# Node-number products for two tiles at once, fewer semaphore waits on VectorE, and shorter ties between gathers and VectorE in a two-layer graph network on one core

## The chip, the cores and the metric

The kernel runs on one core of a Trainium2 chip. The metric is the time of the whole program on the device in microseconds. The core's engines are TensorE (PE in the profile; PEld is its weight loading), VectorE (DVE), ScalarE (ACT), GpSimd (POOL) and SyncE (SP). Each has its own queue of instructions and works through it in order; they wait for each other through semaphores. GpSimd issues the indirect DMAs (gathers), SP most other DMAs.

## The reference

6250 nodes of 256 features, 106250 edges sorted by their target node (100000 random ones and a loop for each node). Layer one is a relational message layer, layer two a graph attention layer of four heads; each is added to its input and normalised.

```python
# layer one
S = feat[src]
msgs = edge_nn(S, W_rel[rel], b_rel[rel])        # relu(relu(S W^T + b) W^T + b), two relations
agg = segment_sum(msgs, dst)
gates = agg @ W_ih.T + b_ih + b_hh               # i, f, g, o
hn = sigmoid(o) * tanh(sigmoid(i) * tanh(g))
x1 = layernorm(x + mlp(hn))                      # W1, W2, W3
# layer two (edges of x1, and a second loop for each node)
h = (x1 @ W).reshape(n, 4, 64)
e = leaky_relu(a_src[src] + a_dst[dst], 0.2)
ex = exp(e - segment_max(e, dst)[dst])
alpha = ex / (segment_sum(ex, dst)[dst] + 1e-16)
out = segment_sum(h[src] * alpha, dst)
y = relu(layernorm(out + bias + x1) * ln_gamma + ln_beta)
return layernorm(x1 + y)
```

## The kernel before

**Tiles, windows, groups, pairs.** The 100000 edges other than the loops are cut into 782 tiles (`TC`) of 128 edges, one edge a partition. Seven tiles (`WT`) make a window, two windows a group (`NG` groups, 56). A group's edges end in at most 128 consecutive nodes. The first window's seven tiles fall into the lower 64 of them (`low_s`), the last four into the upper 64 (`high_s`), and the three between (`MID`, tiles 7 to 9) into any. A group also looks at the first tile of the next one, so it has `GS` = 15 tiles. Groups go in pairs through layer two's weights; the last four go alone.

**Layer one** (in `fast`, from line 1847). For each tile GpSimd gathers 128 rows of 256 numbers from a table of finished messages into a buffer `G`, and TensorE sums them to their target nodes as a product with a one-hot matrix (`sum0`, L2175, accumulated in `fps`). When a group is summed, `turn` (VectorE L1924, L1928; TensorE's transposes L1939; VectorE's copy L1942 to `faT`) hands it to `update`, which runs the gates and the dense layers for up to four groups, and stores the rows of layer two. For the first six groups, ten of the fourteen tiles have been gathered before the loop begins (60 gathers, L1605); only four tiles a group come late.

**Layer two** (from line 2256). GpSimd gathers a row of 260 numbers for each tile (features and the four logits of the source node) into `G[w]`. ScalarE copies the logits out (L2626, L2618). `ahead` makes each edge's node numbers: SP loads the pair's target slots, repeated on every partition (`dB`), VectorE compares them with the partition's number (`ohT`, L2338, 128 x 1920 in bf16), TensorE multiplies each of the 15 tiles' 128 x 128 of `ohT` with the group's `node3` (three bf16 parts of eight numbers a node, 24 columns; L2345), and VectorE adds the three parts (L2355). `weights` turns logits into attention weights through running maxima (L2385 to L2409). `weighted` (L2424, L2429, L2430) multiplies the gathered rows by the weights into `gw`, TensorE sums `gw` by node (L2546), and `finish` normalises and stores a group (L2444 to L2495).

**The order.** Each layer is one loop over steps; a step issues one gather, then the summing of the tile four steps back (`LAG`), then `run.step()`, in which chains of work (`turn`, `update`, `ahead`, `weights`, `finish`) go on by one piece each; a `yield n` in a chain means "n steps later". What is written first stands first in an engine's queue. A step in layer one has the number n of its gather in the loop, which starts at n = 60; in layer two it has the tile's number t, and gathers begin at t = 21.

**The ties.** GpSimd's gathers would run ahead as far as the buffers let them. `Pace` ties them: after each step it notes the last VectorE instruction written so far (`passes`), and `hold(move, n, ahead)` makes gather n wait for the instruction noted `ahead` steps earlier. In layer one `ahead` is `AHEAD0`; in layer two it is `AHEAD1` plus the larger of 0, 42 - (t - 21) // 6 and 21 - (782 - t) // 2 (L2602), so that the tie starts 42 steps looser and tightens until t = 273, and loosens again over the last 42 tiles.

**VectorE's waits for gathers.** `gw` (L2430) reads a window's seven gathered tiles. Each of those gathers signals one of eight semaphores, and L2430 waits for them. The logits of these same rows have gone through ScalarE (L2626) and the whole chain of `weights` before.

Of the kernel before, what the change touches and what calls it, by code (L numbers as in the profile page):

```python
# [42 lines left out]
P = 128  # L43
# [3 lines left out]
H = 4  # L47
# [17 lines left out]
BF16 = mybir.dt.bfloat16  # L65
WT = 7
# [3 lines left out]
GS = 2 * WT + 1  # L70
# [14 lines left out]
AHEAD_G = range(AHEAD_W // 2)  # L85
LATE = 3
CR = 16 * WT
AHEAD0 = 2 * WT
AHEAD1 = WT + 1
NOROW = NP + P // 2 - 1  # L90
SORTED = "the fast path runs only where the chip has found the edges sorted"

# [1547 lines left out]
def fast(  # L1640
# [46 lines left out]
    def at(ap, offset, dims):  # L1687
        return bass.AP(tensor=ap.tensor, offset=ap.offset + offset, ap=dims)
# [35 lines left out]
    class Steps:  # L1724
# [18 lines left out]
        def finish(self):  # L1743
            while self.chains:
                self.step()
# [510 lines left out]
    with (  # L2256
# [45 lines left out]
        def ahead(pair, box):  # L2302

            cut = ring(ep, [P, P + 1], F32, "cut", 3)
            of = ring(ep, [P, 2 * GS, 2 * H], F32, "of", 3)
            box.update(cut=cut, of=of)
            i0, n = pair[0] % 2, len(pair)
            if i0 == 0:
                box["dB"] = ring(ep, [P, 2, GS * P], BF16, "dB", 1)
            else:  # L2310
                box["dB"] = boxes[pair[0] - 1]["dB"]
            dB = box["dB"][:, i0 : i0 + n, :]
            nc.sync.dma_start(
                dB.rearrange("p i e -> p (i e)"),
                at(slots, pair[0] * GS * P, [[0, P], [1, n * GS * P]]),
            )
            if pair in pairs[:2]:
                for i, g in enumerate(pair):
                    nc.sync.dma_start(
                        cut[i * GS * H : (i + 1) * GS * H, :],  # L2320
                        at(cuts, tiles_in(g)[0][0] * P, [[P, GS], [0, H], [1, P + 1]]),
                    )
            else:
                o = pair[0] % 2 * GS * H
                n = ((len(pair) - 1) * GS + len(tiles_in(pair[-1])[1])) * H
                pc = ring(tps, [P, P + 1], F32, "turn", 2)
                nc.tensor.matmul(
                    pc[:n, :],
                    pick[:, pair[0] % 8 // 2, o : o + n],
                    cut_all[:, pair[0] // 8, :],  # L2330
                    start=True,
                    stop=True,
                )
                nc.scalar.copy(cut[:n, :], pc[:n, :])
            yield 12 if len(pair) > 1 else 8
            for i, g in enumerate(pair):
                ohT = ring(ep, [P, GS, P], BF16, "ohT", 2)
                nc.vector.tensor_scalar(  # L2338
                    ohT.rearrange("p j e -> p (j e)"), dB[:, i, :], iota_p, None, op0=OP.is_equal
                )  # L2340
                yield 2
                n = len(tiles_in(g)[1])
                pn = ring(ops, [P, GS, 3, 2 * H], F32, "pn", 2)
                for j in range(n):
                    nc.tensor.matmul(  # L2345
                        pn[:, j, :, :].rearrange("p c a -> p (c a)"),
                        ohT[:, j, :],
                        node3[:, g, :, :].rearrange("p c a -> p (c a)"),
                        start=True,
                        stop=True,  # L2350
                    )
                    if j == WT:
                        yield 1
                yield 1
                nc.vector.tensor_reduce(  # L2355
                    of[:, i * GS : i * GS + n, :],
                    pn[:, :n, :, :].rearrange("p j c a -> p j a c"),
                    axis=AX.X,
                    op=OP.add,
                )  # L2360
                yield 1
# [56 lines left out]
        def weighted(g, w, o, n, of, ex, top):  # L2418

            if g not in ohs:  # L2420
                ohs[g] = ring(ep, [P, (2 * WT - 2) * LOW + 3 * P], F32, "oh1", 2)
                one_hot(ohs[g], g, slot, MID[1])
            gw = ring(ep, [P, WT if n > 1 else 1, D + 2 * H], F32, f"gw{min(n, 2)}", 4)[:, :n, :]
            nc.vector.tensor_mul(  # L2424
                gw[:, :, HA:],
                top[:, o : o + n, :],
                first[:, WT * w : WT * w + n, None].to_broadcast([P, n, H]),
            )
            nc.scalar.copy(gw[:, :, D:HA], ex[:, o : o + n, :])  # L2429
            nc.vector.tensor_mul(  # L2430
                gw[:, :, :D].rearrange("p j (h f) -> p j h f", h=H),
                of[:, :n, :D].rearrange("p j (h f) -> p j h f", h=H),
                ex[:, o : o + n, :, None].to_broadcast([P, n, H, F]),
            )
            return gw

        def finish(g, ps):
# [73 lines left out]
        pair_of = {g: p for p in pairs for g in p}  # L2511
        boxes = {p[0]: {} for p in pairs}
        sums, queue, read, ohs, k3s, left, written = {}, [], set(), {}, {}, {}, []
        results = {}

        def sum1():

            while late and len(queue) < 8:
                piece = late.pop(0)
                g, w, o, n = piece[:4]  # L2520
                gw = weighted(*piece)
                queue.extend((g, WT * w + j, gw[:, j, :]) for j in range(n))
            if not queue:
                return
            g, t, gw = queue[0]
            if g not in sums and g >= 2 and g - 2 not in read:
                return
            queue.pop(0)
            if g not in sums:
                sums[g] = ring(eps, [P, D + 2 * H], F32, "fps1", 2)  # L2530
                left[g] = len(tiles_in(g)[1])
                u = everyone
                if g % 2 == 0:
                    k3s[g // 2] = ring(fp, [P, 2, 3, D], F32, "k3", 2)
                of = k3s[g // 2].rearrange("p i c f -> p i (c f)")
                if len(pair_of[g]) == 1:
                    nc.sync.dma_start(of[:, g % 2, :], kept[g // 2, :, g % 2, :])
                elif g % 2 == 0:
                    nc.sync.dma_start(of, kept[g // 2])
            begins = left[g] == len(tiles_in(g)[1])  # L2540
            left[g] -= 1
            j = t - 2 * WT * g
            to, cols = place(j, MID[1])
            ohj = ohs[g][:, cols]
            ends = left[g] == 0 or j in (WT - 1, TC - 1 - 2 * WT * g)
            nc.tensor.matmul(sums[g][to, :], ohj, gw, start=begins, stop=ends)  # L2546
            if left[g] == 0:
                run.start(finish(g, sums[g]), 1)

        def aheads():  # L2550
            for pair in pairs:
# [42 lines left out]
        while t < TC + LAG or late or queue or run.chains:  # L2594
            if EARLY <= t < TC:
                w = t // WT
                if t % WT == 0:
                    G[w] = ring(rowsp, [P, WT * HA], F32, "G", 10).rearrange(
                        "p (j f) -> p j f", f=HA
                    )  # L2600
                move = gather(G[w][:, t - WT * w, :], rows1, idx1[:, t : t + 1])
                pace.hold(move, t, AHEAD1 + max(0, 6 * WT - (t - EARLY) // 6, 3 * WT - (TC - t) // 2))  # L2602
            k = t - LAG
            if 0 <= k < TC:
                if k < EARLY:
                    complete(k)
                w = k // WT
                g = w // 2
                pair = pair_of[g]
                box = boxes[pair[0]]  # L2610
                if k % (2 * WT) == 0:
                    if g == pair[0]:
                        box["e"] = ring(ep, [P, 2 * GS, H], F32, "e", 3)
                    if g:

                        old = pair_of[g - 1]
                        ob = boxes[old[0]]
                        nc.scalar.copy(  # L2618
                            ob["e"][:, old.index(g - 1) * GS + 2 * WT, :], G[w][:, 0, D:HA]
                        )  # L2620
                        if old is not pair:
                            run.start(weights(old, ob))
                if k == tiles_of(w)[0][-1]:
                    o = pair.index(g) * GS + WT * (w % 2)
                    own = len(tiles_of(w)[0])
                    nc.scalar.copy(box["e"][:, o : o + own, :], G[w][:, :own, D:HA])  # L2626
                    if w == NW - 1:
                        run.start(weights(pair, box))
            sum1()
            if len(queue) + W8 * len(late) > 3 * W8 or t % 7 == 0 or t >= TC - 4 * WT:  # L2630
                sum1()
            run.step()
            pace.passes()
            t += 1
# [62 lines left out]
```

## Time and profile before

| | |
|---|---|
| median of 9 runs | 2182.18 us (2180.41 to 2187.76) |
| the profiled execution | 2182.2 us, its span 2180.4 us |
| granted TensorE clock, mean | 0.843 (0.96 from 237 to 1131 us, 0.71 to 0.74 after 1159 us) |

Busy microseconds of each engine in four stretches (layer one's gathers; layer two until 1500 us; the rest of its gathers; the tail):

| stretch, us | PE | DVE | ACT | POOL |
|---|---|---|---|---|
| 237 to 1131 | 775.1 | 364.6 | 216.5 | 678.3 |
| 1159 to 1500 | 207.2 | 260.8 | 61.2 | 256.0 |
| 1500 to 2131 | 361.0 | 499.6 | 125.5 | 478.4 |
| 2131 to 2181 | 18.6 | 33.5 | 10.4 | 0.0 |

A profile row for a group of instructions gives its line, its engine, its operation, what it writes and reads, and a count; then busy us, mean ns of one, and the idle time of the engine just before these instructions with what ended it. A row of the timeline gives start and duration in us, and in square brackets the idle time before it and what ended it; "issue" is time in which the engine waited for nothing that the profile shows. A row of the chain gives start, duration and the work that the end was waiting for.

### The profile page before, as it was taken

To read this page: it belongs to the slowest core of one execution; us is meant where nothing else is said; L and a number is where in the kernel's file an instruction comes from. 1 tells how busy PE (TensorE), PEld (TensorE's weight loads), DVE (VectorE), ACT (ScalarE), POOL (GpSimd) and SP (SyncE) were. 2 spreads that over 40 slices of the span, in tenths; PEclk is the share of its full clock that TensorE was granted. 3 is DMA by queue.
4 is the path that set the end of the run, shared out by engine and by line. 5 is a ranking of instruction groups with operands and counts; after the bars stand their busy time and mean duration, and the time that the engine had idled before them with its cause. 6 is when DMAs were issued, how large, how long until landed. Compare 5 with 4: busy or idle time off the path is not lost.

```text
span 2180.4 us, 23269 instructions
## 1 busy us (share of the span) xinstructions
PE 1587.1 (73%) x6390; PEld 849.6 (39%) x6390; DVE 1319.2 (61%) x3622; ACT 499.4 (23%) x1538; POOL 1543.8 (71%) x1610
## 2 busy tenths in 40 slices
PE   8988998788888888788886665565564656555554
PEld 5656543333333333333454333233332333333332
DVE  8854354434343433434443788888887777778786
ACT  3333132122221222122351121221211112121212
POOL 2465677777777777777777777777777777777770
PEclk9999999999999999999996776777776767676777
DMA  5356645455554555445555555655555555555551
GB/s 158 118 170 174 188 145 184 140 145 172 169 166 122 165 167 167 137 148 173 185 156 175 164 166 161 178 161 158 181 162 160 164 160 164 160 170 153 164 160 38
DMA packets 146105, 346.12 MB, mean 159 GB/s; under 512 B 36154, under 2 KB 66720, under 8 KB 145965
## 3 DMA queue, kind: packets, MB, share of 16 engines
q0 software_dynamic: 76048, 207.99, 34.7%
q1 hardware_dynamic: 67741, 133.51, 17.7%
q10 hardware_dynamic: 2176, 3.05, 0.4%
q8 instruction: 52, 0.85, 0.2%
q14 instruction: 88, 0.72, 0.1%
HBM read 291.90 MB, written 52.52 MB: 158 GB/s over the span
## 4 chain that ended last, share of the span: by engine, by line
PE 27%; DVE 22%; DMA 18%; issue 11%; POOL 9%; ACT 5%; DVEq 0%; POOLq 0%; ACTq 0%
DMA G<-parts,fidx 10%; PE fps L2175 9%; POOL G L1717 9%; DMA G<-rows,fidx 8%; DVE gw L2430 5%; PE fpg L2006 5%; PE fps L2546 4%; DVE oh L1832 4%; PE fpg L2092 2%; PE fps L2288 1%; PE fpm L1571 1%; DVE fst L2476 1%; PE fpg L2054 1%; ACT fy L2484 1%; DVE ohT L2338 1%
## 5 line engine op out<-in xcount | busy, mean ns | idle before, releaser
L1717 POOL DMA_INDIRECT G<-rows,fidx x761 | 730.5, 960 | 235.2 <-issue 130.9
L1717 POOL DMA_INDIRECT G<-parts,fidx x722 | 693.4, 960 | 230.5 <-issue 156.0
L2546 PE MATMUL fps<-gw,oh 128*64 128x264 f32 (+1 forms) x1674 | 472.0, 472 | 187.9 <-DVE gw L2430 187.9
L2175 PE MATMUL fps<-G,oh 128*64 128x257 f32 (+1 forms) x1674 | 495.3, 413 | 123.3 <-DMA G<-parts,fidx 108.7
L2546 PEld LDWEIGHTS fps<-gw,oh 128*64 128x64 f32 (+1 forms) x1674 | 243.4, 178 | 335.9 <-DVE gw L2430 202.5
L2175 PEld LDWEIGHTS fps<-G,oh 128*64 128x64 f32 (+1 forms) x1674 | 207.9, 154 | 388.7 <-DMA G<-parts,fidx 187.6
L2430 DVE TENSOR_TENSOR gw<-G,bank 128x1792 f32<-128x1792 f32 (+1 forms) x167 | 248.9, 1490 | 57.6 <-ACT gw L2429 52.9
L2006 PE MATMUL fpg<-faT,fWihT 128*128 128x512 f32 (+2 forms) x432 | 171.1, 520 | 0.2 <-DVE faT L1942 0.2
L1832 DVE TENSOR_TENSOR oh<-bank,fslot 128x448 f32<-128x448 f32 (+2 forms) x318 | 156.5, 547 | 8.9 <-ACT bank L2409 5.8
L1924 DVE TENSOR_SCALAR kind<-fps 128x1 f32<-128x1 f32 x112 | 12.4, 152 | 214.2 <-PE fps L2175 214.2
L1571 PE MATMUL fpm<-fWrT,fhT 128*128 128x256 f32 x392 | 94.6, 393 | 13.1 <-DVE fms L1579 13.1
L2126 DVE COPY nd<-hr 128x4 f32<-128x4 f32 x53 | 9.7, 184 | 152.6 <-ACT hr L2098 152.6
L2006 PEld LDWEIGHTS fpg<-faT,fWihT 128*128 128x128 f32 x432 | 71.3, 191 | 67.2 <-issue 56.4
L1557 PE MATMUL fph<-fxc,fWrT 128*128 128x512 f32 (+1 forms) x208 | 89.9, 582 | 5.4 <-DMA fWrT<-in_WrT_dram 4.6
L1605 POOL DMA_INDIRECT G<-parts,fidx x60 | 61.2, 1019 | 43.2 <-DVE fms L1579 18.9
L2345 PE MATMUL pn<-node,ohT 128*128 128x24 bf16 x837 | 41.0, 180 | 67.6 <-DVE ohT L2338 67.6
L1571 PEld LDWEIGHTS fpm<-fWrT,fhT 128*128 128x128 f32 x392 | 75.3, 196 | 32.0 <-DVE fms L1579 11.8
L2478 ACT ACTIVATE frs<-fmv,eps_c 128x1 f32<-128x1 f32 x112 | 32.9, 294 | 238.5 <-DVE gw L2424 153.2
L2484 ACT ACTIVATE fy<-fy,frs 128x256 f32<-128x256 f32 x112 | 66.9, 597 | 87.1 <-DVE frs L2481 86.9
L2345 PEld LDWEIGHTS <-ohT 128*128 128x128 bf16 x837 | 34.1, 103 | 109.0 <-DVE ohT L2338 75.4
L2378 PE MATMUL turn<-fident,e 128*120 128x128 f32 (+2 forms) x30 | 11.6, 388 | 88.2 <-ACT e L2618 88.2
L2092 PE MATMUL fpg<-Wx,fyT 128*128 128x264 f32 x224 | 71.2, 445 | 3.0 <-ACT fyT L2083 3.0
(348 smaller groups left out, 1969.9 us busy)
## 6 DMA issues: line engine op xcount, KB each, us to landing
dB<-slots SPq DMA_DIRECT2D x26, 960.0 KB, 6.1
kept<-keep SPq DMA_DIRECT2D x26, 768.0 KB, 5.2
k<-kept SPq DMA_DIRECT2D x26, 768.0 KB
loop<-parts SPq DMA_DIRECT2D x55, 256.0 KB, 2.9
parts<-fms SPq DMA_DIRECT2D x49, 256.0 KB, 2.4
G<-parts,fidx POOLq DMA_INDIRECT x782
G<-rows,fidx POOLq DMA_INDIRECT x761
out_dram<-fy SPq DMA_DIRECT2D x56, 128.0 KB, 2.9
```

What stands on the lines that cost most here:

```text
L1557: nc.tensor.matmul(ph[:, :cols], WrT_s[:, r, k, m * P : (m + 1) * P], xc[:, k, :cols], start=(k == 0), stop=(k == 1),)
L1571: made = nc.tensor.matmul(pm[:, r, :], hT[:, r, k, j * P : (j + 1) * P], WrT_s[:, r, k, :], start=(k == 0), stop=(k == 1),)
L1605: nc.gpsimd.indirect_dma_start(out=of[:, n % WT, :D], out_offset=None, in_=parts0[: 2 * P * block, :], in_offset=bass.IndirectOffsetOnAxis ...
L1717: return nc.gpsimd.indirect_dma_start(out=to_tile, out_offset=None, in_=table, in_offset=bass.IndirectOffsetOnAxis(ap=idx, axis=0),)
L1832: nc.vector.tensor_tensor(to[:, o : o + len(js) * n].rearrange("p (j s) -> p j s", s=n), iota_s[:, None, cols].to_broadcast([P, len(js), n ...
L2006: nc.tensor.matmul(pg[:, :cols], WihT_s[:, k, c * P : (c + 1) * P], aT[:, k, :cols], start=(k == 0), stop=(k == 1),)
L2092: nc.tensor.matmul(ph[u, :], hs[i][:, k, u], Wx[:, k, :], start=(k == 0), stop=(k == 1))
L2175: nc.tensor.matmul(sums[g][to, :], ohj, got[t], start=begins, stop=ends)
L2345: nc.tensor.matmul(pn[:, j, :, :].rearrange("p c a -> p (c a)"), ohT[:, j, :], node3[:, g, :, :].rearrange("p c a -> p (c a)"), start=True ...
L2430: nc.vector.tensor_mul(gw[:, :, :D].rearrange("p j (h f) -> p j h f", h=H), of[:, :n, :D].rearrange("p j (h f) -> p j h f", h=H), ex[:, o ...
L2484: nc.scalar.activation(y, y, AF.Identity, bias=m, scale=r)
L2546: nc.tensor.matmul(sums[g][to, :], ohj, gw, start=begins, stop=ends)
```

## The change

Three edits.

1. **Products for two tiles.** `dB` and `ohT` hold 10 tiles' columns instead of 15. Columns 0 to 4 hold, in the lower 64 partitions, tiles 0 to 4 and, in the upper 64, tiles 10 to 14; columns 5 and 6 hold tiles 5 and 6 below and -1 above; columns 7 to 9 hold tiles 7 to 9 in all partitions. The load of `dB` becomes three, each to 64 partitions. For each group ScalarE copies `node3` into `node2[g % 4]`, a matrix of 48 columns whose first 24 are zero above and whose last 24 are zero below. One product of a column of `ohT` with it writes the results of tiles j and j + 10. A group has 10 products instead of 15 (five of 48 columns, five of 24), split 6 and 4 by the `yield`. Four `node2` buffers are zeroed and `dB` is filled with -1 once, at the start of layer two.
2. **VectorE's waits.** L2430's dependence on the gathers of its window is declared absent.
3. **Ties.** `AHEAD0` from 14 to 7, `AHEAD1` from 8 to 5.

```diff
-AHEAD0 = 2 * WT
-AHEAD1 = WT + 1
+AHEAD0 = WT
+AHEAD1 = WT - 2
...
-                box["dB"] = ring(ep, [P, 2, GS * P], BF16, "dB", 1)
+                box["dB"] = ring(ep, [P, 2, MID[1] * P], BF16, "dB", 1)
...
-            nc.sync.dma_start(
-                dB.rearrange("p i e -> p (i e)"),
-                at(slots, pair[0] * GS * P, [[0, P], [1, n * GS * P]]),
-            )
+            for ps, c0, j0, jn in (
+                (low_s, 0, 0, MID[1]),
+                (high_s, 0, MID[1], GS - MID[1]),
+                (high_s, MID[0], MID[0], MID[1] - MID[0]),
+            ):
+                nc.sync.dma_start(
+                    dB[ps, :, c0 * P : (c0 + jn) * P],
+                    at(slots, (pair[0] * GS + j0) * P, [[0, LOW], [GS * P, n], [1, jn * P]]),
+                )
...
-                ohT = ring(ep, [P, GS, P], BF16, "ohT", 2)
+                halves = node2[g % 4]
+                for h, ps in enumerate((low_s, high_s)):
+                    nc.scalar.copy(
+                        halves[ps, h, :], node3[ps, g, :, :].rearrange("p c a -> p (c a)")
+                    )
+                ohT = ring(ep, [P, MID[1], P], BF16, "ohT", 2)
...
-                for j in range(n):
-                    nc.tensor.matmul(
-                        pn[:, j, :, :].rearrange("p c a -> p (c a)"),
-                        ohT[:, j, :],
-                        node3[:, g, :, :].rearrange("p c a -> p (c a)"),
-                        start=True,
-                        stop=True,
-                    )
-                    if j == WT:
+                po = pn.rearrange("p j c a -> p j (c a)")
+                for j in range(MID[1]):
+                    if j < GS - MID[1]:
+                        to, of_n = po[:, j : MID[1] + j + 1 : MID[1], :], halves
+                    elif j < MID[0]:
+                        to, of_n = po[:, j, :], halves[:, 0, :]
+                    else:
+                        to, of_n = po[:, j, :], node3[:, g, :, :].rearrange("p c a -> p (c a)")
+                    nc.tensor.matmul(to, ohT[:, j, :], of_n, start=True, stop=True)
+                    if j == MID[1] // 2:
                         yield 1
...
-            nc.vector.tensor_mul(
+            made = nc.vector.tensor_mul(
...
+            for move in brought.get(w, [])[:n]:
+                tc.declare_no_dep(
+                    made.ins, move.ins, reason="the weights come from logits of these rows"
+                )
...
+        node2 = [ep.tile([P, 2, 6 * H], BF16, name=f"node2_{i}") for i in range(4)]
+        for halves in node2:
+            nc.vector.memset(halves, 0.0)
+        nc.vector.memset(ring(ep, [P, 2, MID[1] * P], BF16, "dB", 1), -1.0)
...
+                brought.setdefault(w, []).append(move)
```

More of the change, by code (lines that the diff above doesn't have):

```diff
@@ L2513, in fast @@
         sums, queue, read, ohs, k3s, left, written = {}, [], set(), {}, {}, {}, []
-        results = {}
+        results, brought = {}, {}
         def sum1():
```

## The prediction

> **What bounds the kernel now.** I read the page's busy shares first, then the costliest groups, then GpSimd's timeline, then the chain that ended last.
>
> ```profile
> PE 1587.1 (73%) x6390; PEld 849.6 (39%) x6390; DVE 1319.2 (61%) x3622; ACT 499.4 (23%) x1538; POOL 1543.8 (71%) x1610
> L1717 POOL DMA_INDIRECT G<-rows,fidx x761 | 730.5, 960 | 235.2 <-issue 130.9
> L1717 POOL DMA_INDIRECT G<-parts,fidx x722 | 693.4, 960 | 230.5 <-issue 156.0
> ```
>
> No engine looks full, but GpSimd's 71% hides that each gather is followed by some 0.30 us in which it waits for nothing named ("issue"): (730.5 + 235.2) / 761 = 1.27 us a gather. The two rows make 1483 x 1.27 = 1883 us of the 2180.4 us span. GpSimd's timeline has the next gather 1.25 us after the last one nearly everywhere from 237.7 us to the final one at 2128.9 us. Only five breaks are longer than 0.5 us: one gather that took 2.31 us at 296.7, the change of layers at 1153.8 to 1159.4 us, and waits that ended at 1460.3, 1463.9 and 1493.1 us. So GpSimd's queue sets the time, and the chain confirms both ends of it: layer one's last gather and layer two's last gather are on it, with their tails (29 us to the next layer's start, 50 us to the end) hanging on them.
>
> ```profile
> 1130.94 4.54 DMA G<-parts,fidx
> 2127.66 2.67 DMA G<-rows,fidx
> ```
>
> A stall of GpSimd therefore reaches the end whole, and work of the other engines counts only where it stalls GpSimd.
>
> **The ties.** A gather of loop number n waits until VectorE has passed step n-14 (now n-7) in layer one. I took, for each gather, the VectorE instruction that the changed tie names, and its end in this trace. From 350 us to the end of layer one every gather was issued at least 0.75 us (mostly 4 us or more) after it: no stall. At the start of layer one it isn't so. There the first 24 steps (groups 0 to 5, four late tiles each) carry ten gathered-ahead tiles a group besides, TensorE is the slow one, and VectorE waits for it:
>
> ```profile
> 256.60 0.94 POOL L1717 DMA_INDIRECT G<-parts,fidx  x1 [0.30 <-PE fps L2175]
> 261.58 0.95 POOL L1717 DMA_INDIRECT G<-parts,fidx  x1 [0.31 <-issue]
> 262.26 0.42 DVE L1942 COPY faT<-fpg 128x256 f32<-128x256 f32 x1 [3.21 <-PE fpg L1939]
> 268.29 0.42 DVE L1942 COPY faT<-fpg 128x256 f32<-128x256 f32 x1 [2.06 <-PE fpg L1939]
> ```
>
> Gather n=96 went out at 261.58 us. Its tie moves from step 82 to step 89, whose last VectorE instruction is group 5's L1942, ended at 268.29 + 0.42 = 268.71 us. Gather n=92 (256.60) gets group 4's, ended at 262.68 us, a deficit of 6.1 us; n=96 has the largest, 7.1 us, and no later one exceeds it. From release to a held gather the trace shows 0.27 us (below), so GpSimd falls back by 268.71 + 0.27 - 261.58 = **7.4 us**. Is it made up? GpSimd has no faster pace than 1.25 us. TensorE takes these rows 16 us after the issue of n=96 and 8 to 12 us after the issue of n=110 to 130; with 2.8 us for landing (the least distance from issue to matmul in the trace) it would wait 2 to 3 us at most in between, and by 335 us it waits for each gather anyway. Nothing of layer one's VectorE or TensorE program changes, so I take all 7.4 us, over layer one's last gather into layer two.
>
> In layer two the tie goes from 8 steps to 5, plus a margin that shrinks from 42 steps to none by gather t=273. VectorE lags after the start and catches up; the tie binds already:
>
> ```profile
> 1455.69 0.95 POOL L1717 DMA_INDIRECT G<-rows,fidx  x1 [0.30 <-ACT frs L2479]
> 1458.19 0.95 POOL L1717 DMA_INDIRECT G<-rows,fidx  x1 [0.30 <-issue]
> 1460.29 0.95 POOL L1717 DMA_INDIRECT G<-rows,fidx  x1 [1.15 <-DVE frs L2481]
> 1463.87 0.94 POOL L1717 DMA_INDIRECT G<-rows,fidx  x1 [1.38 <-issue]
> 1493.06 0.94 POOL L1717 DMA_INDIRECT G<-rows,fidx  x1 [1.72 <-DVE frs L2481]
> ```
>
> The L2481 that released t=256 ended at 1460.02 us; 1460.29 is 0.27 later. Three stalls cost 2.10 - 1.25 = 0.85, 1.07 (t=258, whose semaphore had to see the gather of 1451.9 us land) and 1.41 us, together 3.3. With the new tie that same L2481 holds t=253 (issued 1455.69): 4.6 us late; the next pair's, ended 1492.79, holds t=277 (issued 1487.90). Carrying the delay forward and dropping the old stalls that it covers leaves **+3.75 us** with VectorE as it was. Against it stands what VectorE saves before those points.
>
> **The node-number products.** Removed per group: a third of ohT (L2338), 5 of 15 products (L2345, about 0.18 us each but overlapped; TensorE waits there for ohT, so nothing), 40% of dB's bytes. Added: two ScalarE copies a group, 60 more loads on SP, five fills.
>
> ```profile
> L2338 DVE TENSOR_SCALAR ohT<-dB,fiota_p x56: 695/716/933, 1187.8 to 2125.3; 128x1920 bf16<-128x1920 bf16 x56
> L2137 ACT COPY node<-nd x56: 199/210/212, 315.7 to 1160.3; 128x24 bf16<-128x24 bf16 x56
> L1787 DVE MEMSET node<- x1: 618/618/618, 209.7 to 209.7; 128x672 uint32 x1
> ```
>
> ohT at 1280 elements: all proportional gives 716 x 2/3 = 477 ns, a saving of 0.24; with a fixed part as long as the smallest VectorE instruction (152 ns, L1924) 528 ns, a saving of 0.19. I take 0.20. Eighteen run before 1460 us, twenty before 1493: 3.6 and 4.0 us, all of it VectorE's pace there (83% busy, its pair takes 33.3 us against GpSimd's 35.4). That would bring the +3.75 to about 0. The copies cost up to 2 x 0.21 a group in ScalarE's order; where VectorE waits for what stands behind them they eat the saving whole, elsewhere ScalarE is idle (23% busy). Ends: +3.75 without any gain; 0 with all of it; and -2.3 if VectorE gained over 5 us, since then the two old stalls at ties (0.85 and 1.41) go as well. I take **+1.0**, near the full saving, since ScalarE stands idle for 1.6 to 1.7 us on average before its L2391 and L2626 (42.4 / 26 and 188.1 / 111).
>
> [...]
>
> ohT also blocks GpSimd directly. A gather that begins under it ends 0.82 us after it:
>
> ```profile
> 1680.83 0.71 DVE L2338 TENSOR_SCALAR ohT<-dB,fiota_p 128x1920 bf16<-128x1920 bf16 x1
> 1681.12 1.25 POOL L1717 DMA_INDIRECT G<-rows,fidx  x1 [0.30 <-issue]
> 1684.02 0.95 POOL L1717 DMA_INDIRECT G<-rows,fidx  x1 [0.30 <-issue]
> ```
>
> 1681.12 + 1.25 - (1680.83 + 0.71) = 0.83, and 1.25 - 0.95 = 0.30 us lost. Some 17 gathers lose 0.16 to 0.42 us in this way (the first of each pair from 1620 us on). An ohT shorter by 0.20 returns up to 17 x 0.20 = 3.4 us, nothing if the copies shift it against the gathers. I take **-2.5**.
>
> The loads: one dB load of 960 KB lands in 6.1 us and is wanted 12 steps later (15 us); now three of 64 partitions carry 590 KB, each issue about 0.34 us of SP (the k and out rows), which spends 512 us waiting for ScalarE at L2495. Covered; uncovered it would be 0.7 us a pair once, on the k load behind it. [...] The fills (five, at most 1.2 us for dB's 1280 words by L1787's 618 ns for 672, and four small ones) fall into VectorE's 6.7 us of idling for srcb at 1163 to 1169.7 us: nothing, or 1.8 us if that gap were gone.
>
> The products now wait for ScalarE's copies, and L2546 stands behind them on TensorE. Group two's copies stand right behind an e copy (L2626) that waits for a gather. That costs VectorE's lead, not GpSimd, as long as the new tie keeps its 3.1 us of margin (1600 to 2000 us).
>
> **VectorE's own waits left out.** 328 semaphore waits at L2430 go (30 come for dB). They run under the instruction before them; against the usual start, 0.08 us before its end, they delay what follows by 0.15 us in all. Bounds 0 and -0.15: nothing.
>
> **Sum.** 2180.4 + 7.4 + 1.0 - 2.5 = 2186.3 us span; the profiled execution took 2182.2, 1.8 more than its span: **2188.1 us**. The median of the runs, 2182.18, is the same as that execution's.
>
> **Rivals.** (a) *Nearly nothing*: VectorE gains over 5 us by 1460 us, the ties' stalls shrink by 2.3, the gathers return all 3.4: 2182.2 + 7.4 - 2.3 - 3.4 = 2183.9. For it: VectorE is 83% busy there. Against: ohT gives 4.0 at most before 1493. (b) *Faster*: TensorE's order at the start doesn't hold group 5's L1942 back, the tie finds it done, and layer two's gains stand alone: 2182.2 - 2.3 - 3.4 = 2176.5. It decides once that L1942 ends 7 us earlier against gather n=96; against it, layer one's program is unchanged and VectorE there waits for TensorE (3.21 and 2.06 us above). (c) *Slower still*: the copies eat VectorE's gain and move ohT against the gathers: 2182.2 + 7.4 + 3.75 = 2193.4. For it: ScalarE's waits for gathers (166 us at L2626) now stand ahead of the products; against: a 15 us lead of gathers over use at 1460 us.
>
> **Chances.** A median apart by under 0.2% (4.4 us) can't be told from no change here. Forecast 0.45 (slower), (c) 0.18, (a) 0.22 (same), (b) 0.15. The forecast's own range, with its terms' ends, is 2183 to 2194; for 8 in 10 I reach to 2177 toward (b) and to 2196 toward (c).
>
> **What would show it.** Right: in GpSimd's timeline gaps that sum to about 7 us between 245 and 270 us, released by L1928 and L1942; layer two's first gather near 1168 instead of 1160.7 us; 1.25 us pace from there; ohT near 0.50 us and its gathers near 1.05. Wrong: no gaps at 245 to 270 us, gaps in later steady state, or a tail longer than 51 us after the last gather.

## The result, and the profile after

Each kernel was run several times beside the kernel before on the same chip. The changed kernel takes 2193.31 us (median of 10 runs, 2190.73 to 2196.58), the kernel before 2182.41 us (31 runs, 2178.10 to 2188.35): a ratio of 1.0048, 95% interval 1.0040 to 1.0057. That is 10.5 us more by the ratio, 10.9 by the medians; 2188 us, 5.9 more, was forecast. The profiled execution took 2197.29 us, with a span of 2194.9: it is 4 us above its own median, and part of what its trace shows is that execution's alone.

In short: layer one's shorter tie makes GpSimd wait some 7.6 us at the layer's start, and that is never made up. Layer two's shorter tie uses up what VectorE gains. The shorter ohT gives GpSimd's gathers nothing back, because with the new products it holds more of them.

The busy shares and the costliest groups of the changed kernel (busy us, mean ns of one | idle before, and what ended it):

```profile
PE 1587.7 (72%) x6113; PEld 847.3 (39%) x6113; DVE 1314.4 (60%) x3627; ACT 517.7 (24%) x1650; POOL 1548.0 (71%) x1610
L1717 POOL DMA_INDIRECT G<-rows,fidx x761 | 732.3, 962 | 235.7 <-issue 128.1
L1717 POOL DMA_INDIRECT G<-parts,fidx x722 | 694.6, 962 | 239.9 <-issue 157.3
L2362 PE MATMUL pn<-node,ohT 128*128 128x24 bf16 (+1 forms) x560 | 35.2, 191 | 91.6 <-ACT node L2344 50.7
```

TensorE has fewer products than before (it is busy as long), VectorE is busy 4.8 us less and the DMA moves 11 MB less, and the time still grows. GpSimd's gathers are as many and as long as before; what they wait for has changed. The last row is new: 51 us in which TensorE waits for ScalarE's copies. GpSimd doesn't see them.

GpSimd's timeline of the changed kernel at the start of layer one (start, duration, idle before and what ended it), with the VectorE instruction that the tie of gather n=96 names:

```profile
254.25 0.94 POOL L1717 DMA_INDIRECT G<-parts,fidx  x1 [2.16 <-DVE agg L1928]
257.34 0.95 POOL L1717 DMA_INDIRECT G<-parts,fidx  x1 [2.15 <-issue]
261.39 0.95 POOL L1717 DMA_INDIRECT G<-parts,fidx  x1 [0.59 <-PE fps L2175]
264.54 0.95 POOL L1717 DMA_INDIRECT G<-parts,fidx  x1 [2.20 <-DVE faT L1942]
...
269.88 0.42 DVE L1942 COPY faT<-fpg 128x256 f32<-128x256 f32 x1 [2.06 <-PE fpg L1939]
270.57 1.15 POOL L1717 DMA_INDIRECT G<-parts,fidx  x1 [1.34 <-DVE faT L1942]
```

These are the forecast gaps, at the forecast gathers (n=87, 88, 91, 92, 96): 270.57 is L1942's end, 270.30, plus the 0.27 us from release to gather. With two small ones before them (0.86 at 247.32 and 0.37 at 248.64), less the usual 0.30 each, they sum to 0.56 + 0.07 + 1.86 + 1.85 + 0.29 + 1.90 + 1.04 = 7.57 us.

To find where the rest of the time comes from, I took the issue times of the same gather in two traces and subtracted. One trace against the trace of before, in us (positive: later than before):

```
                              changed  ties only  tie0 back  tie1 back  both back  short ohT
before the ties, n=55            1.19       0.37       1.23       2.33       1.80       0.96
after the start, n=147           7.69       7.63      -0.01       9.05       0.84      -0.33
layer two's first gathers       11.56       7.44      -0.06       9.09       2.65      -0.89
before its ties, t=227          12.86       8.20       1.38       9.24       4.22      -2.40
after its ties, t=279           13.63      12.78      -0.37       5.99       1.61      -5.21
late, t=746                     13.85      13.10       0.01       6.74       0.67      -9.53
```

The first row is no work of the change: executions differ by 1 to 2 us before any tie can bind. The other columns are experiments, told next. The changed kernel's column has four parts: the start of layer one, the slow growth from 7.7 to 12.9, layer two's ties, which add 0.8, and nothing at all from t=279 on, where 2.5 us had been forecast as a gain.

### The profile page after: what moved, and what is told of

Read it like the earlier page. It is cut to its first block, busy times and chain, and to the rows that moved or that the text cites. A ratio compares the mean times of both kernels' runs of the same rounds, so it can differ in the third digit from the quotient of the medians.

```text
span 2194.9 us, 22606 instructions
## 1 busy us (share of the span) xinstructions
PE 1587.7 (72%) x6113; PEld 847.3 (39%) x6113; DVE 1314.4 (60%) x3627; ACT 517.7 (24%) x1650; POOL 1548.0 (71%) x1610
## 4 chain that ended last, share of the span: by engine, by line
DVE 28%; PE 27%; DMA 16%; issue 9%; POOL 7%; ACT 5%; SPq 0%; ACTq 0%; DVEq 0%; POOLq 0%
PE fps L2175 9%; DMA G<-parts,fidx 9%; DVE gw L2441 8%; POOL G L1717 7%; DMA G<-rows,fidx 6%; PE fpg L2006 5%; DVE oh L1832 5%; PE fps L2561 4%; PE fpg L2092 2%; PE fps L2288 1%; DVE fst L2491 1%; PE fpm L1571 1%; DVE ohT L2348 1%; PE fpg L2054 1%; ACT fy L2499 1%
## 5 line engine op out<-in xcount | busy, mean ns | idle before, releaser
L2175 PE MATMUL fps<-G,oh 128*64 128x257 f32 (+1 forms) x1674 | 503.6, 418 | 124.9 <-DMA G<-parts,fidx 107.9
L1832 DVE TENSOR_TENSOR oh<-bank,fslot 128x448 f32<-128x448 f32 (+2 forms) x318 | 156.5, 547 | 7.5 <-ACT bank L2420 4.7
L2362 PE MATMUL pn<-node,ohT 128*128 128x24 bf16 (+1 forms) x560 | 35.2, 191 | 91.6 <-ACT node L2344 50.7
L2362 PEld LDWEIGHTS <-ohT 128*128 128x128 bf16 x560 | 29.7, 107 | 131.1 <-DVE ohT L2348 76.9
```

Source lines behind the costliest of these rows:

```text
L1832: nc.vector.tensor_tensor(to[:, o : o + len(js) * n].rearrange("p (j s) -> p j s", s=n), iota_s[:, None, cols].to_broadcast([P, len(js), n ...
L2175: nc.tensor.matmul(sums[g][to, :], ohj, got[t], start=begins, stop=ends)
L2362: nc.tensor.matmul(to, ohT[:, j, :], of_n, start=True, stop=True)
```

## The experiments

**Both ties undone, one by one, and the ties alone.** Four kernels on one chip. The first three are the changed kernel with these lines back, the fourth the kernel before with the new ties:

```diff
-AHEAD0 = WT          e1: 2 * WT    e2: WT        e3: 2 * WT    e4 (from before): WT
-AHEAD1 = WT - 2      e1: WT - 2    e2: WT + 1    e3: WT + 1    e4 (from before): WT - 2
```

Layer one's tie back (e1):

> The changed kernel with layer one's tie back at 14 steps, all else as changed. Theory T (layer one's tie costs 7.4 us at the start, and it is never made up): the gaps between 245 and 270 us go, 7.4 us less than the changed kernel's 2193.3, about 2186, ratio to before 1.0017. Rival R1 (the products' copies, the split loads and ohT moved under more gathers cost most): 2191 or more, 1.004. Rival R2 (layer two's tie costs most): 2191 or more too.

Layer two's tie back (e2):

> The changed kernel with layer two's tie back at 8 steps, all else as changed. Theory T: layer two's tie costs 0.5 to 1 us net, so 2192 to 2193, ratio 1.0045. Rival R2 (layer two's tie costs its full 3.75 us or more): 2189.5 or less, ratio 1.0033 or less. Rival R1: as T.

Both back (e3):

> The changed kernel with both ties back at 14 and 8: the products for two tiles and the waits left out stand alone. Theory T: 2182.4 + 0 to 3, so 2182 to 2185.5, ratio 1.0000 to 1.0014. Rival R1: about 2190, ratio 1.0035. If ohT's saving reached GpSimd as I had forecast (2.5 us and the old stalls): 2178 to 2180, ratio 0.998 to 0.999.

The ties alone (e4):

> The kernel before with the ties at 7 and 5 alone; products, loads and waits as before. Theory T: 7.4 for layer one and 3.75 for layer two without any gain of VectorE's: 2182.4 + 11.2 = 2193.6, ratio 1.0051. Rival R1 (the products cost most): 2186 or less, ratio 1.0017 or less.

Measured, as ratios to the kernel before (2183.42 us there): e1 1.0002 (0.9993 to 1.0011), e2 1.0036 (1.0022 to 1.0050), e3 0.9996 (0.9987 to 1.0005), e4 1.0051 (1.0038 to 1.0065). With layer one's tie back, the loss is gone; the ties alone lose as much as the whole change (4.6 us of it at layer two's tie, below). R1 and R2 as the main cause fall. In e1's timeline the same gathers go out at the usual pace, n=96 at 263.06 us:

```profile
259.31 0.94 POOL L1717 DMA_INDIRECT G<-parts,fidx  x1 [0.30 <-DVE oh L1832]
260.56 0.95 POOL L1717 DMA_INDIRECT G<-parts,fidx  x1 [0.30 <-DVE agg L1928]
261.81 0.95 POOL L1717 DMA_INDIRECT G<-parts,fidx  x1 [0.30 <-issue]
263.06 0.95 POOL L1717 DMA_INDIRECT G<-parts,fidx  x1 [0.30 <-issue]
```

Corrected for the first row of the table, layer one's tie costs (7.69 - 1.19) - (-0.01 - 1.23) = 7.7 us by n=147 between the changed kernel and e1, and (9.05 - 2.33) - (0.84 - 1.80) = 7.7 us between e2 and e3. By the medians it is 1.0048 - 1.0002 = 10.0 us and 1.0036 - 0.9996 = 8.7 us, with uncertainties of 2.7 and 3.6 us. T's "the rest is small" holds, and its 7.4 lies inside these bounds; but e1 itself came out 3 us below T's 2186 us (ratio 1.0017), outside its own interval.

Layer two's tie shows in GpSimd's timeline from 1430 to 1515 us. The gathers with more than 0.45 us of idle time before them, first in the changed kernel:

```profile
1470.39 0.95 POOL L1717 DMA_INDIRECT G<-rows,fidx  x1 [1.64 <-ACT gw L2440]
1497.52 0.95 POOL L1717 DMA_INDIRECT G<-rows,fidx  x1 [0.98 <-issue]
1502.94 0.95 POOL L1717 DMA_INDIRECT G<-rows,fidx  x1 [1.97 <-DVE frs L2496]
```

and in e4, with the new ties and the old products (its first line is the VectorE instruction that the second waited for, 0.27 us before it):

```profile
1434.84 0.15 DVE L2481 SCALAR_TENSOR_TENSOR frs<-fmv,frs 128x1 f32<-128x1 f32 x1
1435.26 0.94 POOL L1717 DMA_INDIRECT G<-rows,fidx  x1 [1.69 <-DVE frs L2481]
1462.52 1.18 POOL L1717 DMA_INDIRECT G<-rows,fidx  x1 [1.31 <-DVE fy L2490]
1469.10 0.95 POOL L1717 DMA_INDIRECT G<-rows,fidx  x1 [2.90 <-ACT gw L2429]
1496.51 0.94 POOL L1717 DMA_INDIRECT G<-rows,fidx  x1 [1.12 <-issue]
1502.09 0.95 POOL L1717 DMA_INDIRECT G<-rows,fidx  x1 [2.13 <-DVE frs L2481]
```

In e2 and e3 there is no such gather: with the tie at 8 steps and the new products the three stalls of before (3.3 us) are gone altogether. So in the table, between "before its ties" and t=279: -3.3 (e2) and -2.6 us (e3) with the old tie and new products, +0.8 (changed) and -1.7 (e1) with the new tie and new products, +4.6 us (e4) with the new tie and old products. The tie therefore costs 0.8 us against the kernel before, but 4.0 against the same kernel with the old tie (changed less e2; e1 less e3 is 0.9): the new products alone would have ended the old stalls, and the tie uses that up. T's 0.5 to 1 us for e2 isn't what these timelines show, and the medians don't decide it: e2's interval holds T's 1.0045 and R2's 1.0033. The same layer two is 2.5 us apart between the changed kernel and e1, which is also what the medians add to layer one's 7.7. VectorE ends its first L2496 73.6 us after the first gather behind the change of layers in the changed kernel and after 71.3 us in e1; why is open (with layer one's short tie it was 73.6, 73.7 and 74.1, with the long one 71.3, 72.6 and, before, 73.9).

**The waits alone.** The kernel before with only the last part of the change:

```diff
-            nc.vector.tensor_mul(
+            made = nc.vector.tensor_mul(
...
+            for move in brought.get(w, [])[:n]:
+                tc.declare_no_dep(made.ins, move.ins, ...)
```

> The kernel before with VectorE's own waits for gathers left out before the weights, and nothing else. All theories: no more than 0.15 us of VectorE's time, none of it seen by GpSimd: 2182 to 2183, ratio 0.9995 to 1.0005. Were the waits worth something, the stalls at 1460 to 1493 us (3.3 us) would be smaller in its timeline.

This run and all later ones but one fell on another chip, on which the kernel before takes 2762.12 us (2741.20 us in a later set) instead of 2182. Ratios there are to its own runs of the kernel before, and its traces say nothing about ties on the first chip. Measured: 0.9981 (0.9961 to 1.0001). That can't be told from no change, and no gain of the forecast's size (0.15 us) could be. Its timeline can't be held against the stalls at 1460 to 1493 us, since the gathers there don't go back to back (GpSimd is busy 56% of its span, 71% in the kernel before on the first chip).

**A shorter ohT alone.** This undoes everything except VectorE's saving:

```diff
-                ohT = ring(ep, [P, GS, P], BF16, "ohT", 2)
+                ohT = ring(ep, [P, MID[1], P], BF16, "ohT", 2)
-                    ohT.rearrange("p j e -> p (j e)"), dB[:, i, :], iota_p, None, ...
+                    ohT.rearrange("p j e -> p (j e)"), dB[:, i, : MID[1] * P], iota_p, None, ...
-                        ohT[:, j, :],
+                        ohT[:, j % MID[1], :],
```

It was run on the other chip twice, and then on one where the kernel before takes 2181.74 us.

> The kernel before with ohT made for 10 of a group's 15 tiles; the products of the last five take the first five's columns, so five tiles' logits come from wrong nodes. No copies on ScalarE, no split loads, 15 products as before. Theory T (a shorter ohT gives VectorE 2 to 3 us by the ties at 1460 to 1493 us, but gives GpSimd's gathers nothing, since it comes to lie on more of them): 2179.5 to 2182.5. Rival R1 (the copies and loads shift ohT onto the gathers; without them each of the 17 held gathers loses 0.10 instead of 0.30 us): gathers under ohT lose 2 to 3 us in all instead of 6 to 6.5, and the time is 2176 to 2179.

> The kernel before with ohT made for 10 of a group's 15 tiles; the products of the last five take the first five's columns, so five tiles' logits come from wrong nodes. No copies on ScalarE, no split loads, 15 products as before. Theory T (a shorter ohT gives VectorE 2 to 3 us by the ties at 1460 to 1493 us, but GpSimd's gathers nothing): gathers under ohT lose 5 to 7 us as before, 2179.5 to 2182.5, ratio 0.9987 to 1.0000. Rival R1 (the copies and loads shift ohT onto the gathers, and without them the short ohT returns what it blocked, as on the other chip, where the loss went from 7.3 to 2.7 us): they lose 3.5 us or less, 2176 to 2179.5, ratio 0.997 to 0.9987.

> The kernel before with ohT made for 10 of a group's 15 tiles; the products of the last five take the first five's columns, so five tiles' logits come from wrong nodes. No copies on ScalarE, no split loads, 15 products as before. On a chip where the kernel before takes 2182 us and its gathers go back to back: if the copies (or anything else of the products' new form) moved a pair's second ohT onto a gather, then without them the second one holds no gather, the first one's loses 0.10 to 0.17 us, the sum under ohT is 4 us or less, and the time 2176 to 2179.5, ratio 0.997 to 0.9987. If the shorter ohT by itself brings the second one onto a gather, the sum is 5.5 to 7 us as with the products (6.3 to 7.0 in four kernels), and the time 2179.5 to 2182.5. On a chip where the kernel before takes 2740 us or more: 0.996 again, and nothing new.

Measured: 0.9959 (0.9938 to 0.9981) and 0.9962 (0.9945 to 0.9979) on the other chip, and 0.9976 (0.9967 to 0.9985), 2176.73 us, on the last. T's "gives GpSimd's gathers nothing" falls: by itself the shorter ohT is worth 5.0 us by the medians. Two things make it up: gathers under ohT lose 4.0 us less (the table below), and of the old stalls at the ties, 3.3 us, only 0.7 is left in its timeline. ohT is as long as in the changed kernel; the rows of the changed kernel and of this one (ns shortest/median/longest):

```profile
L2348 DVE TENSOR_SCALAR ohT<-dB,fiota_p x56: 542/547/777, 1196.2 to 2138.6; 128x1280 bf16<-128x1280 bf16 x56
```

```profile
L2338 DVE TENSOR_SCALAR ohT<-dB,fiota_p x56: 520/548/781, 1186.3 to 2115.6; 128x1280 bf16<-128x1280 bf16 x56
```

What differs is where it falls. One pair in the changed kernel, its two ohT and the gathers after them:

```profile
2014.30 0.55 DVE L2348 TENSOR_SCALAR ohT<-dB,fiota_p 128x1280 bf16<-128x1280 bf16 x1
2014.57 1.08 POOL L1717 DMA_INDIRECT G<-rows,fidx  x1 [0.30 <-DMA G<-rows,fidx]
...
2024.71 0.55 DVE L2348 TENSOR_SCALAR ohT<-dB,fiota_p 128x1280 bf16<-128x1280 bf16 x1
2024.84 1.23 POOL L1717 DMA_INDIRECT G<-rows,fidx  x1 [0.30 <-DVE fy L2505]
```

and one with the shorter ohT alone:

```profile
2026.68 0.55 DVE L2338 TENSOR_SCALAR ohT<-dB,fiota_p 128x1280 bf16<-128x1280 bf16 x1
2026.96 1.08 POOL L1717 DMA_INDIRECT G<-rows,fidx  x1 [0.30 <-issue]
...
2037.15 0.56 DVE L2338 TENSOR_SCALAR ohT<-dB,fiota_p 128x1280 bf16<-128x1280 bf16 x1
2037.18 0.94 POOL L1717 DMA_INDIRECT G<-rows,fidx  x1 [0.30 <-issue]
```

The pair's first ohT is as forecast in both: its gather takes 1.08 us. The second begins 0.13 us ahead of a gather and holds it for 0.28 us in the one; it begins 0.03 us ahead and holds nothing in the other. A tenth of a microsecond of VectorE's order decides. Over all groups, gathers longer than 1.02 us under ohT, and what they lose beyond 0.95 us (those over 0.98 us counted):

```
                       before  ties only  changed  tie0 back  tie1 back  both back  short ohT
gathers held               22         25       35         36         38         33         18
us lost                  6.45       6.83     6.63       7.01       6.69       6.27       2.43
```

In the two kernels with the old products and in the one with the short ohT, one ohT of a pair lies steadily 0.02 to 0.07 us ahead of a gather and holds none (in all but two at most of the 12 or 13 pairs between 1620 and 2065 us). In all four with the new products it wanders, up to 0.16 us ahead, and from 0.09 on it holds the gather. So the new form takes ohT off its place, and gives back in number what it gains in length. Which part of it does (the copies that the products wait for, the split loads, or the waits left out, which shorten VectorE's order by a few hundredths) wasn't separated.

**Layer one's tie loosened only at its start.** The changed kernel, with

```diff
-                pace.hold(move, n, AHEAD0)
+                pace.hold(move, n, AHEAD0 + (WT if n < 112 else 0))
```

> The changed kernel with layer one's tie at 14 steps for its gathers up to n=111 and at 7 from there on. Theory T (the stall is made at n=83 to 104 alone): the same as with the tie back at 14 throughout, 2182 to 2184, ratio 1.0002. Rival (the tie costs in steady state as well, which the drift from 7.7 to 11.6 us over layer one in the changed kernel's profile would be): 2186 or more, ratio above 1.0015, and the drift of its gathers against the kernel before's from n=150 to 800 is 3 us or more.

> The changed kernel with layer one's tie at 14 steps for its gathers up to n=111 and at 7 from there on. Theory T (the stall is made at n=83 to 104 alone): the same as with the tie back at 14 throughout (ratio 1.0002), 1.0000 to 1.0010. Rival (the tie costs in steady state as well, as the drift from 7.7 to 11.6 us over layer one in the changed kernel's profile would have it): ratio above 1.0015, and a drift of its gathers against the kernel before's of 3 us or more from n=150 to 800.

Both fell on the other chip: 0.9877 (0.9858 to 0.9897) and 0.9914 (0.9895 to 0.9932). Neither theory had a gain there, and they don't test them: on a chip where gathers aren't back to back a stall at 250 us need not reach the end. That the tie need not cost anything after n=112 on the first chip rests on the table: e2 and e4, with the tie at 7, run from 9.05 and 7.63 us after the start to 9.09 and 7.44 at the change of layers, and no gather in between waits longer than usual. The changed kernel, with the same program there as e2, grows from 7.69 to 11.56 in its profiled execution. Part of that is the tie: n=726 is released by an L1942, 0.76 us late,

```profile
1070.19 0.39 DVE L1942 COPY faT<-fpg 128x256 f32<-128x256 f32 x1
1070.86 0.95 POOL L1717 DMA_INDIRECT G<-parts,fidx  x1 [1.05 <-DVE faT L1942]
```

and two other gathers (n=693 and 698) wait 0.72 and 0.09 us more than usual. So the short tie can bind there, and the rival isn't wholly out; the rest of the growth is spread over the execution and isn't explained.

**What makes ohT hold a gather.** Two forms of ohT, both with the old ties and the new products, to see whether a slower ohT still holds a gather. In e10 it writes every second element:

```diff
-                ohT = ring(ep, [P, MID[1], P], BF16, "ohT", 2)
+                ohT = ring(ep, [P, MID[1], P, 2], BF16, "ohT", 2)[:, :, :, 0]
```

> [...] Rival (any VectorE instruction reading dB holds the gather, whatever its speed): the gathers under it take 1.2 to 2 us each, 2195 or more.

In e11 it is made with three operands from group 20 on:

```diff
+                    nc.vector.scalar_tensor_tensor(
+                        same, dB[:, i, :], iota_p, ones[:, 0:1].to_broadcast([P, MID[1] * P]),
+                        op0=OP.is_equal, op1=OP.mult,
+                    )
```

> Both ties back at 14 and 8, products for two tiles, and from group 20 on ohT by an instruction of three operands with one of them 4-byte numbers, as oh's (which holds no gather in any trace here) rather than by the one that holds gathers. Theory: ohT takes about 1.4 us from group 20 on, no gather under it takes more than 1.0 us, so some 5 us of lost gather time go between 1550 us and the end; VectorE has the time there (its pair 33 + 1.7 us against GpSimd's 35.2): 2175 to 2179, ratio 0.9965 to 0.9985. Rival (VectorE, slower by 0.85 us a group, falls behind the gathers and the ties bind, or the tail grows): gaps of GpSimd at the ties after 1600 us or a tail over 53 us, 2182 or more.

Both on the other chip: 0.9982 (0.9958 to 1.0006) and 1.0024 (1.0007 to 1.0041). That a slower ohT holds no gather falls twice; on what holds a gather, e10 fits its rival (any VectorE instruction reading dB, whatever its speed). A pair of lines each, first e10, then e11:

```profile
1804.37 0.94 DVE L2348 TENSOR_SCALAR ohT<-dB,fiota_p 128x1280 bf16<-128x1280 bf16 x1
1804.73 1.36 POOL L1717 DMA_INDIRECT G<-rows,fidx  x1 [0.92 <-DVE fy L2505]
```

```profile
2393.72 1.54 DVE L2352 SCALAR_TENSOR_TENSOR ohT<-dB,fiota_p,ones 128x1280 bf16<-128x1280 bf16 x1
2394.07 2.01 POOL L1717 DMA_INDIRECT G<-rows,fidx  x1 [0.88 <-DVE fy L2510]
```

The slower forms, 0.94 and 1.54 us, hold the gather as the one of 0.55 us does, until 1804.73 + 1.36 - 1805.31 = 0.78 and 2394.07 + 2.01 - 2395.26 = 0.82 us after their end. Gathers under ohT lose 18.8 us in e10 and 34.5 in e11. The longer ohT held it longer (1.36 and 2.01 us for the gathers above, 1.08 and 1.23 in the pair of the changed kernel). e11's third operand was taken for like oh's, and it isn't: oh (L1832) and gw (L2430) read one of their two operands, `bank`, from PSUM, where e11's ones lie in SBUF. In the trace of before, of the gathers that begin at least 0.1 us after such an instruction's start and 0.25 us before its end, none takes more than 1.02 us under oh (0 of 63) and gw (0 of 142), while all do under L2026 (11 of 11), L2019 (5 of 5) and L2490 (6 of 6), whose two inputs lie in SBUF, and under ohT (16 of 16). L1928 has both forms in one line: all three gathers under it are held where the sum that it adds to lies in SBUF (`agg`), and none of seven where it lies in PSUM (`fps`). e10 and e11 agree with these counts: in both, ohT reads SBUF alone. An ohT with its ones in PSUM wasn't tried, so that the operand's place decides is a reading of the counts and not shown by a change of it.

No kernel that computes the whole reference beats the kernel before on the first chip: both ties back is level with it (0.9996).

## Why the prediction was right in its direction, and what was off

- *What bounds the kernel.* Right. TensorE, VectorE and the DMA got less work, and only what GpSimd waited for counted: the new 51 us of TensorE's waits for the copies are nowhere in its timeline.
- *Layer one's tie, +7.4 us, at n=87 to 96, never made up.* Right, place and size: 7.57 us of gaps (from n=83 on), 7.7 twice against the kernels with the tie back, and in e2 and e4 still there at the change of layers. The medians put 9 to 10 us on it, within their uncertainty; what that is more than 7.7 is open.
- *Layer two's tie, +1.0 from +3.75 less VectorE's gain.* Right: +0.8 in the changed kernel's profile. The working holds too: +4.6 with the old products (e4, 3.75 forecast), and VectorE's gain takes nearly all of it. With the old tie VectorE's gain ended the old stalls whole (-3.3 and -2.6 us), where -2.3 and a gain of over 5 us had been taken as the end. The tile numbers that the prediction gives for these gathers (253, 256, 258 and 277) are each one too high, which changes nothing in its sum.
- *ohT's length.* 0.50 forecast, 0.547 measured: against 0.716 before, 0.17 us saved instead of 0.20. Of the two estimates from the 716 ns, 477 all proportional and 528 with a fixed part, the second is the nearer.
- *ohT's hold on the gathers, -2.5.* This is the step that failed. Its price was right: the first gather of a pair fell from 1.25 to 1.08 us, and with ohT shortened alone the gathers under it lost 2.43 instead of 6.45 us. Its clause "nothing if the copies shift it against the gathers" is what came about, with a shift of 0.1 us that I had no number for: 35 gathers are held instead of 22, and they lose 6.63 us instead of 6.45, so the term is +0.2 and not -2.5. Up to t=279 it even cost time: the gathers under ohT lose 1.09 us in the kernel before, 1.98 in the changed one and 0.33 with the short ohT alone; after that it is 5.36, 4.65 and 2.11.
- *Copies, loads, fills and waits: nothing.* Right for their direct cost: the change of layers is as long as before (1165.42 to 1172.29, 6.9 us; before 7.0), and the waits alone can't be told from no change. They are suspects for ohT's shift. The three loads of a pair carry 576 KB in the unit of the 960 KB, not 590, which changes nothing.
- *The sum.* Without the failed -2.5 it would have been 2190.6, 2.7 below the median; these 2.7 us stay open. Rivals (a) and (b) are out: layer one's stall was made and kept. Rival (c) gives the right number, 2193.4, for half the right reason: ohT did move against the gathers, but VectorE's gain wasn't eaten and the 3.75 us weren't paid.
- *The signs.* Layer two's first gather came at 1172.29 us and not near 1168, by the growth over layer one that e2 and e4 don't show. Of the signs of being wrong, three late waits in layer one's steady state (1.6 us) are in the profile; the tail is 52.1 us (before, 51.5).

## What to carry to other kernels

Where one queue runs back to back to the end, a tie that makes it wait is priced by its worst moment (here n=96, at the end of 7.57 us of gaps), and a start-up in which the follower is late costs its whole deficit for good (7.7 us here, still there at the change of layers in e2 and e4): look for that moment before tightening a tie that has slack everywhere else. An instruction that blocks the queue is priced by its length times how often it falls on it, and a change that shortens it can also move it (here from 0.716 to 0.547 us, and from 22 gathers held to 35): measure the shortening alone before crediting it.

## What the runs showed of the hardware

In the traces at the pace of 1.25 us a gather, one that begins within 0.08 us of ohT's start is not held; those that begin from 0.09 us on, while 0.25 us of it are left, are, until 0.81 to 0.82 us after its end (0.78 to 0.82 with the slower forms of e10 and e11).

The second chip was a surprise: the same kernel before takes 2741 to 2762 us there. The page of the waits-only kernel on it, and GpSimd's group at the change of layers, which in the kernel before on the first chip idles 4.7 us:

```profile
PE 1590.4 (58%) x6390; PEld 883.2 (32%) x6390; DVE 1323.8 (48%) x3622; ACT 496.8 (18%) x1538; POOL 1541.6 (56%) x1610
...
PE 31%; DVE 28%; another core or an unknown queue 25%; issue 8%; ACT 4%; DMA 0%; ACTq 0%; SPq 0%; DVEq 0%
```

```profile
L2106 POOL DMA_INDIRECT rows<-rows_l,tail_i x1 | 1.0, 1002 | 46.3 <-ACT keep L2099 46.3
```

The engines' work is the same, to 1% (TensorE's weight loads, 4% more, aside), but there are 80 stretches of 2 to 16 us, 488 us in all (240 to 1430 and 1560 to 2700 us), in which TensorE, VectorE and ScalarE all stand still while GpSimd mostly goes on. Three quarters of the DMA's completions are missing from that trace (6519 recorded for the gathers, 25403 before on the first chip), so what ends these pauses can't be read, and it stays open. There the changed kernel with a loose start was 0.9 to 1.2% faster than the kernel before, and the change of layers idles 27.6 and 27.7 us in it instead of the 46.3 above: which of its parts does that wasn't separated.
